# Key norms of a windowed attention: broadcast by matmul, or through memory

## The chip, the cores and the metric

The kernel runs on one core of a Trainium2 chip. The core has TensorE (PE, with weight loads shown apart as PEld), VectorE (DVE), ScalarE (ACT), GpSimd (POOL) and SyncE (SP), which here only issues transfers. The engines run side by side and wait for each other through semaphores; each works through its own instructions in order. SBUF is the core's working memory of 128 partitions (rows), PSUM the memory that TensorE writes to, and beside them lies the device's main memory. The metric is the device's time for one execution in microseconds.

## The reference

x has 2048 tokens of 128 features. It passes through a stack of six layers, then one block of linear attention and feed-forward, then the same stack again with the same weights; each result is added to x, the stack's by half. One layer of the stack is local attention and a feed-forward block with a gate:

```python
def attn_layer(x, Wqkv, qs, ksc, Wo):
    q, k, v = jnp.split(x @ Wqkv, 3, -1)            # 16 heads of 64
    q, k, v = (sh(q), sh(k), sh(v))
    q = l2norm(q) * qs
    k = l2norm(k) * ksc                             # t / max(norm, 1e-12)
    q = q * cos * scale + rotate_half(q) * sin * scale
    k = k * cos * inv + rotate_half(k) * sin * inv
    out = local_attention(q, k, v)                  # windows of 32, one window back
    return out.transpose(0, 2, 1, 3).reshape(b, n, INNER) @ Wo
def ffn_layer(x, g, bln, W1, b1, W2, b2):
    a, gate = jnp.split(layernorm(x) @ W1 + b1, 2, -1)
    return a * gelu(gate) @ W2 + b2
```

The part that matters here is `l2norm(k)`: every key (one head, one token) is divided by its own norm. For the queries the division is done later, in the scale of the exponential.

## The kernel before

Everything is float32 and kept with features on partitions and tokens along the free dimension. Each of the twelve layer passes (`2 * DEPTH`) is cut into eight chunks of `AC` = 256 tokens. A chunk takes four steps, and a step handles 128 tokens and eight heads of attention. The stages of one chunk are:

- `project` (four groups g, L270 on): TensorE projects q and k (p, L286); VectorE multiplies by the rotary tables (prod, L295); GpSimd adds the two halves into the tiles abq and abk (L301); ScalarE squares p (sq, L307) and GpSimd adds the squares (L321). A tile abk holds two groups, thus eight heads: [128, 2, 2, 256]. Its 128 partitions are four heads of 32 rows, the first index is the half of the 64 features, the second the group. There are three buffers of abk.
- `square_sums` (L329): TensorE sums the squares per head and token into ss, with key heads in rows 64 to 71 and 96 to 103.
- `norms` (L400 to L408): ScalarE and VectorE turn ss into the inverse norms rn, one row per head, 256 tokens.
- `query_norms` (L416, L422) brings the query part of rn to the layout rq, tokens on partitions.
- `scale_keys` (L430, L436), for each half g2 of the heads: each key's row of rn has to meet the 32 rows of its head. Two matmuls with a selection matrix of zeros and ones (`sel_r`) write the repeated rows r into two PSUM buffers, and VectorE multiplies abk by them, four heads at a time.
- `gather` (L387, L393): SP copies abq and abk into the layout hq and hk, in which a head's 64 features lie together. For keys it issues four copies per half.
- `similarities` (sim, L466 and L476) on TensorE, with the maxima taken by VectorE (L488, L489); `exponentials` (L501) on ScalarE; `normalised` (L511, L513): a reciprocal on VectorE, a product on GpSimd; `transposed` (te L526, eT L532); `values` (av L553, oT L560 and L562); `output` (y L569, xf L578). `values_windows` copies v into vw with eight DMAs per 128 tokens (L365 to L368).
- `feed_forward` (pf L603, gate L609, h L614, yf L622) runs on 512 tokens, once every eight steps.

The order of work is written out by hand. `POS` gives each stage a list of places (step, position), counted from the first step of its chunk or block; a stage that is a generator is cut at its `yield`s, and each piece has its own place. The pieces of all layers and chunks are sorted by step, then by position, and emitted in that order, so the same order holds on every engine and in SP's queue. Positions only rank the pieces within a step. Semaphores are put in by the framework where data or buffers demand them.

PSUM serves two buffers for sim, one for ss, and five small ones that all other matmul results, r included, take in turn.

Of the kernel before, what the change touches and what calls it, by code (L numbers as in the profile page):

```python
# [8 lines left out]
F32 = mybir.dt.float32  # L9
BF16 = mybir.dt.bfloat16  # L10
AF = mybir.ActivationFunctionType
ALU = mybir.AluOpType
# [3 lines left out]
P = 128  # L16
# [6 lines left out]
CH = 512  # L23
NCH = N // CH
AC = 256
# [5 lines left out]
HID = 512  # L31
LN_EPS = 1e-5
POS = {
    "tabq": [(-10, 141)],
    "tabk": [(-9, 110)],
    "ss": [(-7, 142)],
    "vwin": [(1, 8)],
    "gq0": [(-5, 13)],
    "gq1": [(-3, 49)],
    "e0": [(0, 76)],  # L40
    "e1": [(0, 77)],
    "nrm": [(1, 10)],
    "qn": [(-2, 106)],
    "ek": [(-1, 73)],
    "proj": [(-9, 135), (-8, 33), (-8, 36), (-8, 37), (-8, 39), (-8, 101)],
    "vproj": [(-2, 24), (-2, 71)],
    "norms": [(-4, 38), (-4, 43), (-4, 63)],
    "sk0": [(-3, 69), (-3, 70)],
    "sk1": [(-1, 119), (-1, 136)],
    "te": [(2, 46), (2, 47)],  # L50
    "av": [(2, 132), (2, 177), (2, 178)],
    "out": [(4, 92), (4, 115)],
    "sim": [(0, 50), (0, 53), (0, 54)],
    "ff": [(11, 99), (12, 30), (12, 130), (13, 21), (13, 94), (14, 139), (15, 124), (15, 149),
        (16, 12), (17, 87), (17, 122), (18, 14), (18, 45), (18, 52), (18, 184), (21, 107),
        (21, 167)],
    "ff2": [(12, 15), (12, 80), (13, 95), (14, 58), (14, 60), (14, 79), (15, 91), (16, 40),
        (16, 58), (16, 147), (16, 182), (16, 187), (16, 191), (17, 34), (17, 111), (17, 121),
        (17, 157)],
    "ff3": [(10, 171), (10, 172), (10, 174), (10, 181), (10, 183), (10, 184), (11, 25), (11, 35),  # L60
        (11, 57), (11, 68), (11, 86), (11, 100), (11, 103), (11, 104), (11, 146), (11, 170),
        (11, 170)],
    "start0": [(-16, 180), (-14, 143), (-13, 66), (-11, 67), (-10, 109), (-10, 185)],
    "start1": [(-10, 65), (-9, 134), (-8, 96), (-8, 148), (-6, 20), (-6, 26)],
    "start2": [(-7, 2), (-7, 117), (-6, 6), (-6, 48), (-4, 74), (-4, 176)],
    "start3": [(-6, 28), (-4, 32), (-4, 44), (-4, 75), (-4, 98), (-4, 188)],
    "sums0": [(-9, 105), (-8, 5), (-8, 88), (-8, 123), (-8, 134), (-7, 102), (-7, 118), (-6, 27)],
    "sums1": [(-1, 137), (-1, 145), (0, 56), (0, 114), (1, 116), (1, 133), (2, 154), (2, 172)],
    "sums2": [(1, 189), (2, 173), (2, 178), (2, 192), (3, 144), (3, 153), (4, 125), (4, 126)],
    "sums3": [(3, 179), (4, 11), (4, 19), (4, 42), (4, 82), (4, 83), (4, 84), (4, 128)],  # L70
    "kv": [(5, 1)],
    "outs0": [(5, 3), (5, 4), (5, 7), (5, 9), (5, 22), (5, 85), (6, 18), (6, 113), (6, 164),
        (7, 17), (7, 90), (7, 129), (7, 163), (7, 190)],
    "outs1": [(6, 61), (11, 78), (12, 131), (13, 120), (13, 127), (13, 140), (13, 160), (14, 59),
        (14, 186), (15, 29), (15, 41), (15, 112), (15, 138), (15, 165)],
    "outs2": [(5, 23), (13, 51), (13, 62), (13, 169), (14, 31), (14, 55), (14, 166), (14, 168),
        (15, 44), (15, 64), (15, 159), (16, 150), (16, 158), (17, 97)],
    "outs3": [(5, 175), (15, 93), (16, 16), (16, 81), (16, 151), (16, 160), (16, 161), (17, 72),
        (17, 89), (17, 108), (17, 152), (17, 156), (17, 162), (18, 155)],
}  # L80
EXP_LN = "natural_log_exp_and_others"

# [11 lines left out]
def kernel(ctx: ExitStack, tc: tile.TileContext, a: dict, out: bass.AP):  # L94
    nc = tc.nc

    const = ctx.enter_context(tc.tile_pool(name="const", bufs=1))
    work = ctx.enter_context(tc.tile_pool(name="work", bufs=2))
    ps_sim = ctx.enter_context(tc.tile_pool(name="ps_sim", bufs=2, space=PSUM))
    ps_small = ctx.enter_context(tc.tile_pool(name="ps_small", bufs=5, space=PSUM))  # L100
    ps_ss = ctx.enter_context(tc.tile_pool(name="ps_ss", bufs=1, space=PSUM))

    def small(name):
        return ps_small.tile([P, CH], F32, tag="small", name=name)

    def keep(shape, name, dtype=F32, src=None):
        t = const.tile(shape, dtype, name=name)
        if src is not None:
            dims = "abc"[: len(shape) - 1]
            flat = t.rearrange(f"p {' '.join(dims)} -> p ({' '.join(dims)})") if len(dims) > 1 else t  # L110
            if dtype == F32:
                nc.sync.dma_start(flat, src)
            else:
                nc.sync.dma_start(t, src)
        return t

    def load_qk(l, g):
        w = const.tile([P, 4, P], F32, tag=f"wqk{g}", name=f"wqk{g}_{l}")
        nc.sync.dma_start(
            w,  # L120
            a["Wqk"][l % DEPTH].rearrange("p (g f) -> p g f", g=4)[:, g, :]
            .rearrange("p (u f) -> p u f", u=4),
        )
        return w
# [25 lines left out]
    def load_x(f):  # L150
        nc.sync.dma_start(xo[:, f * CH : (f + 1) * CH], a["xT"][:, f * CH : (f + 1) * CH])

    load_x(0)
    sq_consts = keep([P, 5, P], "sq_consts", src=a["squares"].rearrange("p a b -> p (a b)"))
    ident, hmask, rot_m = (sq_consts[:, i, :] for i in range(3))
    sel_r = sq_consts[:, 3:5, :]
    wqk = [load_qk(0, g) for g in range(4)]
    rot = keep([P, 2, 2, AC], "rot", src=a["rot"])
    qks = keep([P, DEPTH, 2, 2], "qks", src=a["qks"])
# [108 lines left out]
    def chunk(l, c):  # L268
        return chunks.setdefault((l, c), {"nm": f"{l}_{c}"})
# [141 lines left out]
    def query_norms(l, c):  # L411
# [10 lines left out]
        nc.vector.tensor_copy(rq.rearrange("p t h -> p (t h)"), nt[:, 0 : 2 * HEADS])  # L422
        d["rq"] = rq

    def scale_keys(l, c, g2):
        d = chunk(l, c)
        rs = [small(f"r_{d['nm']}_{2 * g2 + i}") for i in range(2)]
        for i in range(2):
            rows = slice(64 + 32 * i, 96 + 32 * i)
            nc.tensor.matmul(  # L430
                rs[i][:, 0:AC], sel_r[rows, g2, :], d["rn"][rows, :], start=True, stop=True
            )
        yield
        for i in range(2):
            k = d["k", g2][:, :, i, :]
            nc.vector.tensor_tensor(  # L436
                k, k, rs[i][:, 0:AC].unsqueeze(1).to_broadcast([P, 2, AC]), ALU.mult
            )
        gather(l, c, "k", g2)

    def earlier_keys(l, c):
# [336 lines left out]
    for l in range(2 * DEPTH):  # L778
        base = per * l + (GAP if l >= DEPTH else 0)

        def put(key, t0, fn, *args):

            places = POS[key]
            if len(places) > 1:
                pieces(fn(*args), t0, places)
            else:
                at(t0 + places[0][0], places[0][1], fn, *args)

        put("tabq", base, tables, l, 0)
        put("tabk", base, tables, l, 1)  # L790
        for c in range(NAC):

            t0 = base + STEPS * c
            for g in range(4):
                put("proj", t0 + g, project, l, c, g)
                put("vproj", t0 + g, values_proj, l, c, g)
            for g2 in range(2):
                put("ss", t0 + 2 * g2, square_sums, l, c, g2)
                put("gq" + "01"[g2], t0, gather, l, c, "q", g2)
                put("sk" + "01"[g2], t0, scale_keys, l, c, g2)  # L800
            for t in range(2):
                put("vwin", t0 + 2 * t, values_windows, l, c, t)
                put("out", t0 + 2 * t, output, l, c, t)
            put("norms", t0, norms, l, c)
            put("qn", t0, query_norms, l, c)
            put("ek", t0, earlier_keys, l, c)
            for s in range(STEPS):
                put("sim", t0 + s, similarities, l, c, s)
                put("e0", t0 + s, exponentials, l, c, s, 0)
                put("e1", t0 + s, exponentials, l, c, s, 1)  # L810
                put("nrm", t0 + s, normalised, l, c, s)
                put("te", t0 + s, transposed, l, c, s)
                put("av", t0 + s, values, l, c, s)
        for f in range(NCH):
            key = "ff"
            if l % DEPTH == DEPTH - 1 and f >= 2:
                key = f"ff{f}"
            put(key, base + 8 * f, feed_forward, l, f)
# [15 lines left out]
def _shape_constants():  # L834
# [7 lines left out]
    t = np.arange(AC, dtype=np.float64)[None, :]  # L842
# [16 lines left out]
    c, s = np.diag(back * np.cos(AC * inv)), np.diag(back * np.sin(AC * inv))  # L859
    one = np.block([[c, -s], [s, c]]).reshape(2, 32, 2, 32).transpose(1, 0, 3, 2).reshape(64, 64)  # L860
    rot_m = np.kron(np.eye(2), one)


    i, j = np.arange(WIN)[:, None], np.arange(SK)[None, :]
# [4 lines left out]
    band = band.reshape(P, 2, SK).astype(ml_dtypes.bfloat16)  # L869
    ident_b = np.tile(np.eye(2 * WIN, WIN), (2, 1)).astype(ml_dtypes.bfloat16)  # L870
    r = np.arange(P)
    sel_r = [r[:, None] % 32 == 4 * i + r[None, :] // 32 for i in range(2)]
    squares = np.stack(
        [r[:, None] == r[None, :], r[:, None] // 8 == r[None, :] // 8, rot_m, *sel_r], 1
    ).astype(np.float32)

    sel = np.zeros((P, 3, 32), np.float32)
# [68 lines left out]
```

## Time and profile before

| | |
|---|---|
| runs, median (lowest to highest) | 3536.89 us (3532.78 to 3539.96) |
| profiled execution, its own time | 3536.21 us |
| its span, first to last instruction | 3534.4 us |
| mean granted TensorE clock | 0.981 of full |
| L430 r, matmul instructions on TensorE | 768, busy 145.1 us |
| L430 r, weight loads | 768, busy 66.8 us |
| L436 abk, VectorE multiplies by r | 384, busy 246.7 us |
| hk<-abk, copies issued by SP | 768 of 128 KB |
| hq<-abq, copies issued by SP | 384 of 256 KB |
| vw<-v, copies issued by SP | 768 of 128 KB, 744 of 64 KB |
| mean DMA traffic over the span | 396.13 MB, 112 GB/s |

Busy time of an engine is the time that at least one of its instructions covers. The ends of matmuls are modelled, while their starts are recorded, and weight loads overlap matmuls. A float32 matmul appears as two instructions. "Idle before" is the time that an engine stood ahead of a group of instructions, with what ended it. SPq is SP's queue of transfer issues.

The twelve passes run in two halves of six, and between them lies the linear attention, where little else can run: there TensorE is busy 294.59 of 372 us (1568 to 1940 us of the span).

### The profile page before, as it was taken

What the parts mean: (1) busy time and instruction counts of PE and PEld (TensorE: products, weight loads), DVE (VectorE), ACT (ScalarE), POOL (GpSimd) and SP (SyncE); (2) the same over time, 40 slices, a digit from 0 to 9 for tenths busy, and PEclk for the clock granted to TensorE, in tenths of its full rate; (3) what the DMA queues carried; (4) which work ended last, traced back from release to release, by engine and by line L of the source; (5) the groups of instructions that cost most, each with busy time, mean ns of one, the idle gap of its engine ahead of it and who ended that gap; (6) DMA issues with size and microseconds to landing.
All of it is one profiled execution on the core that took longest, in us unless ns stands there. A gap on an engine that the chain in (4) does not pass through costs nothing.

```text
span 3534.4 us, 154488 instructions
## 1 busy us (share of the span) xinstructions
PE 3392.8 (96%) x64856; PEld 2346.8 (66%) x64856; DVE 2553.6 (72%) x5116; ACT 2738.4 (77%) x8805; POOL 2092.2 (59%) x2195
## 2 busy tenths in 40 slices
PE   7999999999999999999678999999999999999998
PEld 4776776666776677666335777767667666776674
DVE  5777777777777777775336777777777777777774
ACT  4788788878878878887446787888788788788877
POOL 6766666666666566563136666666666666666661
PEclk9999999999999999999788999999999999999999
DMA  4554544444545455444003544545545454544552
GB/s 123 127 127 119 118 120 117 117 122 120 124 115 126 115 122 131 107 115 104 12 12 83 125 123 123 119 114 126 120 122 120 112 127 119 118 121 117 117 123 61
DMA packets 295921, 396.13 MB, mean 112 GB/s; under 512 B 45501, under 2 KB 160953, under 8 KB 295225
## 3 DMA queue, kind: packets, MB, share of 16 engines
q1 hardware_dynamic: 295224, 386.25, 45.3%
q8 instruction: 510, 8.36, 1.0%
q14 instruction: 187, 1.52, 0.1%
HBM read 34.27 MB, written 1.05 MB: 10 GB/s over the span
## 4 chain that ended last, share of the span: by engine, by line
PE 35%; ACT 8%; DVE 6%; issue 1%; POOL 0%; DMA 0%; ACTq 0%; SPq 0%; POOLq 0%; DVEq 0%
PE p L286 7%; ACT e L501 5%; PE av L553 4%; PE y L569 4%; PE pv L345 4%; DVE prod L295 3%; PE sim L476 3%; PE pf L603 2%; PE yf L622 2%; PE te L526 2%; ACT L607 1%; PE r L430 1%; PE ss L329 1%; PE sim L466 1%; DVE eT L532 1%
## 5 line engine op out<-in xcount | busy, mean ns | idle before, releaser
L501 ACT ACTIVATE e<-sim,st,rq 128x64 f32<-128x64 f32 x3072 | 1194.5, 410 | 292.3 <-DVE st L489 288.9
L295 DVE TENSOR_TENSOR prod<-p,tab 128x1024 f32<-128x1024 f32 x768 | 922.3, 1212 | 130.9 <-ACT sq L307 96.1
L513 POOL TENSOR_TENSOR e<-e,st 128x512 f32<-128x512 f32 x384 | 400.5, 1043 | 724.9 <-DVE st L511 697.6
L286 PE MATMUL p<-xa,wqk 128*128 128x256 f32 x3072 | 773.5, 395 | 18.3 <-ACT sq L307 6.3
L301 POOL TENSOR_TENSOR abq<-prod 128x512 f32<-128x512 f32 x384 | 490.2, 1276 | 297.5 <-DVE prod L295 252.9
L501 ACT ACTIVATION_READ_ACCUMULATOR e<-sim,st,rq 128x1 f32 x3072 | 647.9, 211 | 0.0
L307 ACT ACTIVATE sq<-p 128x512 f32<-128x512 f32 x768 | 438.8, 602 | 248.0 <-PE ss L329 101.4
L286 PEld LDWEIGHTS p<-xa,wqk 128*128 128x128 f32 x3072 | 558.2, 191 | 106.5 <-ACT sq L307 9.6
L301 POOL TENSOR_TENSOR abk<-prod 128x512 f32<-128x512 f32 x384 | 487.2, 1269 | 166.6 <-DVE prod L295 89.5
L321 POOL TENSOR_TENSOR sq<-sq 128x256 f32<-128x256 f32 x768 | 546.9, 734 | 0.0
L553 PEld LDWEIGHTS av<-eT,vw 64*64 64x64 f32 x18432 | 401.7, 135 | 171.3 <-DVE st L489 48.0
L553 PE MATMUL av<-eT,vw 64*64 64x32 f32 x18432 | 446.8, 221 | 3.4 <-issue 1.1
L345 PE MATMUL pv<-wv,xa 128*128 128x512 f32 x768 | 413.4, 620 | 19.4 <-ACT gate L609 18.7
L569 PE MATMUL y<-oT,wo 128*128 128x128 f32 x3072 | 395.1, 282 | 0.2 <-DVE oT L562 0.2
L553 PE MATMUL av<-eT,v 64*64 64x32 f32 x6144 | 390.9, 219 | 0.0
L569 PEld LDWEIGHTS y<-oT,wo 128*128 128x128 f32 x3072 | 359.0, 192 | 19.4 <-issue 1.7
L488 DVE TENSOR_REDUCE sim<-sim 128x4 f32<-128x256 f32 x768 | 325.4, 424 | 14.1 <-PE sim L476 14.0
L476 PE MATMUL sim<-hk,hq 64*32 64x64 f32 x24576 | 332.9, 222 | 0.0
L526 PEld LDWEIGHTS te<-sq_consts,e 128*128 128x128 f32 x1536 | 188.5, 141 | 209.4 <-issue 151.6
L553 PEld LDWEIGHTS av<-eT,v 64*64 64x64 f32 x6144 | 325.6, 135 | 0.0
L476 PEld LDWEIGHTS sim<-hk,hq 64*32 64x32 f32 x24576 | 305.6, 105 | 0.2
L603 PE MATMUL pf<-xc,w 128*128 128x512 f32 (+1 forms) x576 | 290.4, 629 | 11.9 <-POOL xc L591 7.5
(141 smaller groups left out, 4549.6 us busy)
## 6 DMA issues: line engine op xcount, KB each, us to landing
hq<-abq SPq DMA_DIRECT2D x384, 256.0 KB
hk<-abk SPq DMA_DIRECT2D x768, 128.0 KB
vw<-v SPq DMA_DIRECT2D x768, 128.0 KB
vw<-v SPq DMA_DIRECT2D x744, 64.0 KB
wqk<-in_Wqk SPq DMA_DIRECT2D x48, 256.0 KB
wv<-in_Wv SPq DMA_DIRECT2D x24, 256.0 KB
wo<-in_Wo SPq DMA_DIRECT2D x12, 512.0 KB
w<-in_W SPq DMA_DIRECT2D x12, 341.0 KB
```

What stands on the lines that cost most here:

```text
L286: nc.tensor.matmul(both[s][:, u, :], wqk[g][:, 2 * s + u, :], xs, start=True, stop=True)
L295: nc.vector.tensor_tensor(prod, both[s].unsqueeze(2).to_broadcast([P, 2, 2, AC]), tabs[l, s].rearrange("p (u v) t -> p u v t", u=2), ALU.mult,
L301: nc.gpsimd.tensor_tensor(d["qk"[s], g // 2][:, :, g % 2, :], prod[:, 0], prod[:, 1], ALU.add)
L307: nc.scalar.activation(sq, both[s], AF.Square)
L321: nc.gpsimd.tensor_tensor(sq[:, 0, :], sq[:, 0, :], sq[:, 1, :], ALU.add)
L345: nc.tensor.matmul(ps, xa[:, ti * P : (ti + 1) * P], wv[j], start=True, stop=True)
L476: nc.tensor.matmul(sims[par][WIN * b : WIN * b + WIN, i, :], d["hq"][rows, 4 * h8 + i, at : at + WIN], d["hk"][rows, 4 * h8 + i, at : at + ...
L501: nc.scalar.activation(e[:, i, par, :], d["sims", step][par][:, i, :], AF.Exp, bias=st8[:, 0, i, par : par + 1], scale=rq[:, i, par : par ...
L513: nc.gpsimd.tensor_tensor(ef, ef, st8[:, 1].rearrange("p i r -> p (i r)").unsqueeze(2).to_broadcast([P, 8, SK]), ALU.mult,)
L553: nc.tensor.matmul(av[u][r : r + 64, m, WIN * b : WIN * b + WIN], d["vs", t][u][b][:, at : at + DH], d["eT", step][64 * u : 64 * u + 64, i ...
L569: nc.tensor.matmul(y[:, 0:P], wo[:, i, :], d["oT", t].rearrange("p h u m q -> p (h u m) q")[:, i, :], start=(i == 0), stop=(i == 7),)
L603: nc.tensor.matmul(ps[s][:r], w1[:, s, j * P : j * P + r], x, start=True, stop=True)
```

## The change

The inverse key norms no longer pass through TensorE. A new stage, `spread_norms`, writes the two times eight rows of rn that belong to keys into a buffer in main memory (two DMAs), and in a second piece reads them back with four DMAs. Each of the four fills 32 partitions and reads the same 4 KB block for every one of them, so each row is read 32 times. The result is a tile rk of [128, 4, 256] in SBUF, of which there is one buffer; the buffer in main memory exists twice.

`scale_keys` is now a single piece without matmul: one multiply of 128 x 1024 elements per half takes eight heads, both inputs in SBUF. The selection matrices `sel_r` and their part of the load of `squares` are gone. `gather` is called as before.

The table `POS` is written anew as a whole; most pieces keep their step and change their position. Those that stand close to the edit are shown here.

```diff
-    "norms": [(-4, 38), (-4, 43), (-4, 63)],
-    "sk0": [(-3, 69), (-3, 70)],
-    "sk1": [(-1, 119), (-1, 136)],
+    "norms": [(-4, 35), (-4, 75), (-4, 111)],
+    "rk": [(-4, 195), (-3, 19)],
+    "sk0": [(-2, 20)],
+    "sk1": [(-1, 83)],
...
-    "proj": [(-9, 135), (-8, 33), (-8, 36), (-8, 37), (-8, 39), (-8, 101)],
+    "proj": [(-9, 137), (-8, 31), (-8, 32), (-8, 33), (-8, 36), (-8, 57)],
...
-    "sim": [(0, 50), (0, 53), (0, 54)],
+    "sim": [(0, 65), (0, 66), (0, 67)],
...
-    "nrm": [(1, 10)],
+    "nrm": [(1, 9)],
...
-    "start0": [(-16, 180), (-14, 143), (-13, 66), (-11, 67), (-10, 109), (-10, 185)],
+    "start0": [(-18, 189), (-15, 77), (-15, 88), (-15, 140), (-12, 30), (-10, 165)],
...
+    dram = ctx.enter_context(tc.tile_pool(name="dram", bufs=2, space=bass.MemoryType.DRAM))
...
+    def spread_norms(l, c):
+
+        d = chunk(l, c)
+        out = dram.tile([2, 2, 4, AC], F32, tag="rk", name=f"rkd_{d['nm']}")
+        for i in range(2):
+            row = 64 + 32 * i
+            nc.sync.dma_start(out[:, i], d["rn"][row : row + 8, :])
+        yield
+        r = work.tile([P, 4, AC], F32, tag="rk", name=f"rk_{d['nm']}", bufs=1)
+        src = out.rearrange("a b j t -> j (a b) t")
+        for j in range(4):
+            nc.sync.dma_start(
+                r[32 * j : 32 * j + 32], src[j : j + 1].to_broadcast([32, 4, AC])
+            )
+        d["rk"] = r
+
     def scale_keys(l, c, g2):
         d = chunk(l, c)
-        rs = [small(f"r_{d['nm']}_{2 * g2 + i}") for i in range(2)]
-        for i in range(2):
-            rows = slice(64 + 32 * i, 96 + 32 * i)
-            nc.tensor.matmul(
-                rs[i][:, 0:AC], sel_r[rows, g2, :], d["rn"][rows, :], start=True, stop=True
-            )
-        yield
-        for i in range(2):
-            k = d["k", g2][:, :, i, :]
-            nc.vector.tensor_tensor(
-                k, k, rs[i][:, 0:AC].unsqueeze(1).to_broadcast([P, 2, AC]), ALU.mult
-            )
+        k = d["k", g2].rearrange("p u i t -> p u (i t)")
+        r = d["rk"][:, 2 * g2 : 2 * g2 + 2, :].rearrange("p i t -> p (i t)")
+        nc.vector.tensor_tensor(k, k, r.unsqueeze(1).to_broadcast([P, 2, CH]), ALU.mult)
         gather(l, c, "k", g2)
...
+            put("rk", t0, spread_norms, l, c)
```

In program order each engine then meets, for one chunk: VectorE finishes rn (step -4); SP issues the writes at the end of that step and the reads early in the next; VectorE multiplies the first half early in step -2, right behind the reciprocal that stands at the head of the step, and the second half in step -1 behind the maxima of sim; SP issues four copies into hk after each.

## The prediction

> **What bounds the kernel now.** I read the busy table first, then busy time by stretches, then who waits for whom, then single lines of the timeline. The page gives the engines over the whole span:
>
> ```profile
> PE 3392.8 (96%) x64856; PEld 2346.8 (66%) x64856; DVE 2553.6 (72%) x5116; ACT 2738.4 (77%) x8805; POOL 2092.2 (59%) x2195
> ```
>
> An average over stages is not a bound, so here are four stretches (columns: span, then busy time of PE, PEld, DVE, ACT, POOL, then granted clock, DMA share, GB/s). 68 us hold eight steps, that is two chunks of attention and one block of feed-forward.
>
> ```profile
> core 0: us, PE busy (x) PEld busy (x) DVE busy (x) ACT busy (x) POOL busy (x), PEclk, DMA share, GB/s
> 180.00:1568.00 1388.00, 1378.39 (x27448) 971.69 (x27447) 1051.23 (x2119) 1129.33 (x3684) 869.04 (x910) 1.00 0.50 120
> 996.00:1064.00 68.00, 67.60 (x1347) 47.65 (x1348) 51.89 (x104) 55.36 (x182) 42.32 (x45) 1.00 0.46 115
> 1568.00:1940.00 372.00, 294.59 (x3431) 169.74 (x3430) 191.58 (x356) 215.02 (x557) 139.43 (x150) 0.85 0.23 55
> 1940.00:3436.00 1496.00, 1485.59 (x29774) 1050.82 (x29773) 1136.60 (x2297) 1210.73 (x3989) 943.62 (x986) 1.00 0.50 120
> ```
>
> In the two steady stretches, 2884 of 3534 us, TensorE lacks 0.4 us of 68 at the full granted clock; ScalarE has 81%, VectorE 76%, GpSimd 62%. Their idle time ends on TensorE or on each other; in 180 to 1568 us the list of waits has one entry for PE matmuls, 9.3 us in all. TensorE sets the pace there. Around the middle (1568 to 1940) it does not.
>
> **A rule that speaks against this.** The Trainium skill, page "Perfetto Trace Analysis", section "Identifying the Most-Contended Engine", says that matmul busy time is a poor measure since matmuls are pipelined, and to look at the weight loads' share. That share is 70% here, which would leave TensorE headroom and make removed matmuls worth little or nothing. So I do not trust the 96% alone and look at starts, which are not modelled:
>
> ```profile
> 1008.01 0.70 PE L430 MATMUL r<-rn,sq_consts 32*128 32x256 f32 x4
> 1008.64 1.13 PE L603 MATMUL pf<-xc,w 128*128 128x512 f32 x2
> 1027.98 0.70 PE L430 MATMUL r<-rn,sq_consts 32*128 32x256 f32 x4
> 1028.61 0.32 PE L553 MATMUL av<-eT,vw 64*64 64x32 f32 x8
> ```
>
> From the first r matmul to the first of the next group it is 0.63 us both times, behind different neighbours. A fixed spacing is TensorE's own time, not a wait. I go by the row.
>
> **What the change removes on TensorE.** Each scale_keys had four r instructions (two matmuls, two passes each). 768 instructions are 192 groups, and they lie here (busy time of L430 alone):
>
> ```profile
> 180.00:1568.00 1388.00, 60.22 (x324) 27.69 (x324) 1.00 0.50 120
> 1940.00:3436.00 1496.00, 65.74 (x352) 30.38 (x352) 1.00 0.50 120
> ```
>
> (324 + 352)/4 = 169 groups are in the paced stretches: 169 x 0.63 = 106.5 us. The other 23 (14.5 us) lie in the start, middle and end, where TensorE is busy 85, 79 and 83%; I count half, 7 us. Together 113 us. Busy time says 145 us, but its modelled ends overlap the next group, so I take the spacing. The weight loads of r (66.8 us) lie inside it and are not counted again.
>
> **What it does to VectorE.** Removed: 384 multiplies, 246.7 us, and 17.5 us waiting in front of them. Added: 192 multiplies of 128x1024.
>
> ```profile
> L436 DVE TENSOR_TENSOR abk<-abk,r 128x512 f32<-128x512 f32 x384 | 246.7, 684 | 17.5 <-PE r L430 11.4
> L295 DVE TENSOR_TENSOR prod<-p,tab 128x1024 f32<-128x1024 f32 x768 | 922.3, 1212 | 130.9 <-ACT sq L307 96.1 <-PE p L286 30.4 <-POOL e L513 0.9
> ```
>
> The nearest row of that size takes 1.21 us, so 192 x 1.21 = 233 us. But L295 and the old L436 take one input from PSUM; the new multiply has both in SBUF. The Trainium skill, page "SBUF — State Buffer", section "Who interferes with whom", says that such an instruction and a GpSimd instruction that reads SBUF exclude each other, whoever starts second waiting for the first to finish. The trace agrees where it has such a pair:
>
> ```profile
> L242 DVE SCALAR_TENSOR_TENSOR xc<-lnt,xc x48: 691/693/1493, 170.6 to 3515.8; 128x512 f32<-128x512 f32 x48
> L301 POOL TENSOR_TENSOR abk<-prod x384: 1252/1267/1712, 20.3 to 3437.5; 128x512 f32<-128x512 f32 x192
> ```
>
> (minimum/median/maximum). The VectorE row with two SBUF inputs goes from 0.69 to 1.49 us at worst, a GpSimd add from 1.27 to 1.71. Bounds for the new multiply: 1.21 us without a clash, 1.21 + 1.27 = 2.48 with a whole GpSimd add in front. GpSimd is busy 62% of the time, so a random start meets half an add in 62% of cases: 1.21 + 0.62 x 0.64 = 1.6 us. I take 1.6: 307 us instead of 264, VectorE +43 us, and at worst +212. Both are hidden under TensorE: with 192/2884 of it in each us, VectorE goes from 51.9 to some 53 us in an eight-step period that shrinks to 65.5, about 81%. If that cover is gone, +43 us is the price.
>
> **The round trip of the norms.** New per chunk: two writes of 8 KB and four reads of 128 KB, all in SP's queue. One issue takes SP 0.6 us, so 3.6 us more on top of 28 x 0.6 = 17 in a chunk of some 33 us. Bytes: 0.54 MB beside 4.1 MB per chunk (120 GB/s x 34 us), DMA share 0.50 to about 0.58. Neither queue nor engines fill. What counts is latency, since the first read waits for both writes to land, and the first multiply waits for the reads.
>
> ```profile
> 1003.39 0.42 DVE L408 SCALAR_TENSOR_TENSOR rn<-rn,ss 128x256 f32<-128x256 f32 x1
> 1012.72 0.20 DVE L511 RECIPROCAL st<-st 128x8 f32<-128x8 f32 x1 [0.37 <-ACT e L501]
> 1014.72 0.75 DVE L614 SCALAR_TENSOR_TENSOR h<-pf,lvec,gate 128x512 f32<-128x512 f32 x1 [1.80 <-ACT gate L609]
> 2085.34 0.61 SPq L393
> 2086.00 3.78 DMA hk<-abk
> 3531.19 0.34 SPq L638 DMA_DIRECT2D out_xT<-xo  x1
> ```
>
> Four transfers of 128 KB: 0.61 + 3.78 = 4.4 us from the issue that is shown to the landing; the nearest row for the reads. Writes to memory: the only row is the output, issued at 3531.19 with the span ending at 3534.4, so at most 3.2 us, plus 0.6 for the second issue; below, one issue and nothing, 1.2. I take 3.0, nearer to the row. Sum 7.4 us (5.6 to 8.2). The time there is: after.py puts the first multiply behind the reciprocal of the second step after rn. In the timeline of before, rn ends at 1003.81 and that reciprocal at 1012.92, 9.1 us, and this is a pair of short steps; others are longer. So it fits, with 0.9 to 3.5 us over. Behind SP's waiting read stand a pair of hq copies and eight vw copies, wanted by sim and av a step or more later.
>
> If it is late, VectorE stands, and behind the multiply stand the two prod of that step, eT and the maxima that ScalarE waits for. The trace shows what TensorE can bear: VectorE stood 1.80 us before L614 at 1014.72, and TensorE had no gap. The second multiply comes over a step later and is covered.
>
> **What is moved.** The first multiply goes from place (-3, 70) to (-2, 20); the second from (-1, 136) to (-1, 83), so the last hk copies start earlier before sim, which moves from (0, 50) to (0, 65). The first move has a cost: abk has three buffers, and GpSimd's add into the next chunk's second abk, place (-2, 36), must wait until the four hk copies that read the old one have landed. Multiply about 1.6 us, then 4.4: it waits some 2 to 3 us once a chunk. Such waits are 43.5 us in all before. GpSimd has 38% of 34 us, 13 us, to spare per chunk, and sums of squares and exponentials are used over half a step later. I cost it at nothing; with that cover gone, each us is 96 us.
>
> Start: the round trip takes about 7 us where the r matmuls took 1. First r at 43.3 us, first sim at 66.2, so most of it is hidden; I put 4 us for it and for the start of the second half. The rest of the new table of places shifts neighbours without adding work; between -10 and +10 us, taken as 0.
>
> **Sum** on the profiled execution, 3534.4 of span plus 1.8 around it = 3536.2: -113 + 4 = -109, 3427. The median of the runs is 3536.9, 0.7 above, so 3428.
>
> **The rivals.**
> 1. *Part of the gain comes back* (0.17). Clashes of VectorE and GpSimd, or GpSimd's wait for hk, leave TensorE standing about 0.5 us per chunk: 96 x 0.5 = 48 us, 3476. For it: a period of 65.5 us leaves ScalarE 10 us and VectorE 12 of idle time, against 13 and 16 now. Against: before shows that TensorE covers waits of this size.
> 2. *Slower: the round trip is late* (0.19). Place: the first multiply of each chunk. TensorE's idle there must exceed 109/96 = 1.14 us per chunk to cancel the gain; with 1.8 us of cover, the reads must land about 3 us behind the reciprocal, a round trip of some 12 us instead of 7.4. At 13 us TensorE loses about 2.1 us per chunk: 3428 + 202 = 3630; at 12.5 it is about 3580. For it: a write to memory and a read of one 4 KB block by 32 rows are in no row of the trace, and SP takes everything in order. Against: twice my sum for the transfers would be needed.
> 3. *No change* (0.03): another engine takes over at 68 us per period. ScalarE would have to, with 55.4 us of work; 3537.
>
> **Numbers.** The forecast itself has 0.61, range 3405 to 3455 (gain from 121 + 10 to 82). About 0.2% is what can be told from no change, 7 us. Faster: 0.61 + 0.17 = 0.78, within 0.03, slower 0.19. The likeliest is 3428; the range 3403 to 3530 takes in rival 1 and leaves out rival 2 and the edges.
>
> **What would show it.** No L430 rows; an eight-step period of about 65.5 us with TensorE over 99% busy; the multiply at 1.2 to 2.5 us, mean near 1.6; VectorE's waits on DMA rk few and short; GpSimd's waits on hk rising to 200 us or more without TensorE standing. Wrong would be: a long list of VectorE waits on rk, gaps on TensorE behind eT or prod, or a period still near 68 us.

## The result, and the profile after

The changed kernel takes 3645.5 us in the median (3634.1 to 3649.1), the kernel before 3537.0 us beside it. The ratio is 1.0302, 95% interval 1.0277 to 1.0327: about 107 us slower, where 109 us of gain were forecast. In what follows a ratio is turned into microseconds by the 3537 us of before.

The busy table of the page after, and the four stretches of before again (columns: span, busy time of PE, PEld, DVE, ACT, POOL, then granted clock, DMA share, GB/s):

```profile
PE 3328.7 (91%) x64088; PEld 2297.7 (63%) x64088; DVE 2575.6 (71%) x4924; ACT 2748.6 (75%) x8805; POOL 2253.8 (62%) x2195
```

```profile
180.00:1568.00 1388.00, 1315.04 (x26360) 923.82 (x26359) 1030.25 (x1979) 1097.80 (x3573) 913.88 (x886) 0.98 0.54 131
996.00:1064.00 68.00, 65.14 (x1331) 45.97 (x1330) 52.34 (x100) 55.23 (x182) 44.77 (x42) 1.00 0.55 135
1568.00:1940.00 372.00, 289.19 (x3625) 171.25 (x3625) 198.70 (x362) 223.79 (x572) 149.76 (x152) 0.88 0.28 69
1940.00:3436.00 1496.00, 1402.11 (x28201) 984.23 (x28199) 1099.65 (x2118) 1170.67 (x3837) 980.43 (x950) 0.99 0.54 131
```

TensorE lost 64 us of busy time over the span, but it now stands: 1388 - 1315 = 73 us in the first steady stretch, where before it stood 10, and 94 us in the second, also against 10. The granted clock, 1.00 in both stretches before, is 0.98 and 0.99. Over the whole span TensorE is idle 308 us instead of 136 (the idle time in front of its matmuls, summed over the trace). So -64 busy and +172 idle make +108. What it waits for is in GpSimd's groups and in the rows of the new multiply (first lines: busy, mean ns | idle before it, by what ended it; then the multiply's duration minimum/median/maximum, and VectorE's idle before it):

```profile
L302 POOL TENSOR_TENSOR abk<-prod 128x512 f32<-128x512 f32 x384 | 502.4, 1308 | 728.6 <-DMA hk<-abk 573.4 <-DVE prod L296 34.2 <-DVE st L497 25.4
L322 POOL TENSOR_TENSOR sq<-sq 128x256 f32<-128x256 f32 x768 | 593.9, 794 | 0.0
L446 DVE TENSOR_TENSOR abk<-abk,rk x192: 1167/1320/2367, 52.3 to 3573.9; 128x1024 f32<-128x1024 f32 x192
...
  DMA rk<-rkd: 2.1, 3
```

```profile
PE ss L330 <- POOL sq L322: 59.4, 54, 6.8
PE pf L611 <- POOL xc L599: 52.5, 35, 4.6
PE pv L346 <- ACT gate L617: 46.7, 48, 1.8
PE pf L611 <- ACT oT L568: 30.5, 42, 4.4
PE av L561 <- DMA vw<-v: 20.0, 32, 1.3
```

The multiply, once its place comes, waits for the new transfer 2.1 us in all: the round trip itself is on time. GpSimd, though, waits 573 us for the hk copies to leave its abk buffers (before: 43.5 us), 6 us per chunk. Behind that add stand GpSimd's sums of squares and the feed-forward's xc, and for these TensorE waits 59 and 53 us over the whole span. The same waits in the kernel before:

```profile
POOL abk L301 <- DMA hk<-abk: 43.5, 27, 4.1
PE ss L329 <- POOL sq L321: 10.2, 7, 2.7
PE pf L603 <- POOL xc L591: 7.5, 2, 4.6
```

One such place, from the timelines of SP, VectorE and GpSimd in the kernel after (start, duration):

```profile
1003.82 1.43 DVE L446 TENSOR_TENSOR abk<-abk,rk 128x1024 f32<-128x1024 f32 x1
1002.45 1.17 SPq L388 DMA_DIRECT2D hq<-abq  x2
1003.67 0.72 SPq L366 DMA_DIRECT2D vw<-v  x1
...
1009.32 0.59 SPq L369 DMA_DIRECT2D vw<-v  x1
1010.02 2.52 SPq L394 DMA_DIRECT2D hk<-abk  x4
1015.72 1.27 POOL L302 TENSOR_TENSOR abk<-prod 128x512 f32<-128x512 f32 x1 [5.93 <-DMA hk<-abk]
```

The multiply ends at 1005.25, but its hk copies go out at 1010.02, since eight window copies stand ahead of them in SP's queue, and those stood behind the hq copies, which wait for sim (573.7 us of SP's waiting over the span). GpSimd's add, for which the buffer must be free, comes at 1015.72 after 5.93 us of standing. Over all chunks the median time from the end of the multiply to the issue of its first hk copy is 1.69 us for the first half of the heads and 4.70 us for the second. Before, SP stood ready: its first copy goes out 0.57 us ahead of the end of the pair of multiplies.

### The profile page after: what moved, and what is told of

Its sections match the earlier page's. It is cut to its first block, busy times and chain, and to the rows that moved or that the text cites. A ratio compares the mean times of both kernels' runs of the same rounds, so it can differ in the third digit from the quotient of the medians.

```text
span 3642.3 us, 153352 instructions
## 1 busy us (share of the span) xinstructions
PE 3328.7 (91%) x64088; PEld 2297.7 (63%) x64088; DVE 2575.6 (71%) x4924; ACT 2748.6 (75%) x8805; POOL 2253.8 (62%) x2195
## 4 chain that ended last, share of the span: by engine, by line
PE 47%; ACT 17%; DVE 13%; POOL 9%; DMA 7%; issue 4%; SPq 4%; POOLq 0%; ACTq 0%; DVEq 0%
PE p L287 10%; ACT e L509 9%; DVE prod L296 6%; PE av L561 6%; PE y L577 6%; PE pv L346 4%; PE pf L611 4%; DMA hk<-abk 4%; PE sim L484 4%; PE yf L630 3%; POOL abk L302 3%; POOL sq L322 3%; PE te L534 3%; SPq L394 2%; DMA vw<-v 2%
## 5 line engine op out<-in xcount | busy, mean ns | idle before, releaser
L302 POOL TENSOR_TENSOR abk<-prod 128x512 f32<-128x512 f32 x384 | 502.4, 1308 | 728.6 <-DMA hk<-abk 573.4
L287 PE MATMUL p<-xa,wqk 128*128 128x256 f32 x3072 | 782.1, 398 | 7.9 <-DVE xa L243 4.0
L521 POOL TENSOR_TENSOR e<-e,st 128x512 f32<-128x512 f32 x384 | 475.7, 1239 | 288.7 <-DVE st L519 223.0
L302 POOL TENSOR_TENSOR abq<-prod 128x512 f32<-128x512 f32 x384 | 508.0, 1323 | 178.7 <-DVE prod L296 160.0
L322 POOL TENSOR_TENSOR sq<-sq 128x256 f32<-128x256 f32 x768 | 593.9, 794 | 0.0
L611 PE MATMUL pf<-xc,w 128*128 128x512 f32 (+1 forms) x576 | 304.2, 655 | 84.4 <-POOL xc L599 52.5
L570 DVE COPY oT<-av 128x256 f32<-128x256 f32 x384 | 162.1, 422 | 255.1 <-PE av L561 252.5
```

The lines of the kernel that those rows point to most:

```text
L287: nc.tensor.matmul(both[s][:, u, :], wqk[g][:, 2 * s + u, :], xs, start=True, stop=True)
L302: nc.gpsimd.tensor_tensor(d["qk"[s], g // 2][:, :, g % 2, :], prod[:, 0], prod[:, 1], ALU.add)
L322: nc.gpsimd.tensor_tensor(sq[:, 0, :], sq[:, 0, :], sq[:, 1, :], ALU.add)
L521: nc.gpsimd.tensor_tensor(ef, ef, st8[:, 1].rearrange("p i r -> p (i r)").unsqueeze(2).to_broadcast([P, 8, SK]), ALU.mult,)
L611: nc.tensor.matmul(ps[s][:r], w1[:, s, j * P : j * P + r], x, start=True, stop=True)
```

## The experiments

The runs tell these theories apart. Theory A: the new table of places makes the hk copies late in SP's queue. Theory T or L: the round trip costs, by its transfers and SP's time (T), or because something is late through it (L). Theory G: ScalarE's gate is the next bound, right behind TensorE, so that removed matmuls bring little. Theory P, called B in the first expectations: VectorE and GpSimd hold each other up. Theory C: the added transfers fill the DMA engines. G was formed after the first four runs, whose expectations don't speak of it. The short diffs are against the kernel named ahead of them.

**e1_vw_places**, against after: the window copies behind the hk copies.

```diff
-    "vwin": [(1, 68)],
+    "vwin": [(0, 21)],
```

> The changed kernel with one place moved: the eight vw copies go from place (1, 68) to (0, 21), so that they no longer stand in SP's queue right ahead of the hk copies. Theory A (the hk copies start late because of what stands ahead of them in SP's order, the abk buffers come free late, GpSimd waits, TensorE starves): from the end of the multiply to the first hk issue 1.7 and 4.7 us fall to under 1 us, GpSimd's wait for hk falls from 575 us to under 250, time 3430 to 3520. Theory B (VectorE's multiply with two SBUF inputs and GpSimd shut each other out): nothing of that matters, 3620 to 3650. Theory C (the added transfers fill the DMA engines): 3620 to 3650.

Measured 3578.2 us, ratio 1.0113 (1.0098 to 1.0128). The first hk copy now goes out 0.03 us after the multiply, GpSimd's wait for hk falls from 573 to 124 us, and 67 us come back, which neither B nor C foresaw:

```profile
POOL abk L302 <- DMA hk<-abk: 124.0, 99, 3.4
```

The direction of A is right and its size was too large: 40 us above before remain, and the 109 us of gain are still missing.

**e2_matmul_at_places**, against after: the matmuls and the multiplies from PSUM at the new places, no round trip.

```diff
-    "rk": [(-4, 195), (-3, 19)],
-    "sk0": [(-2, 20)],
-    "sk1": [(-1, 83)],
+    "sk0": [(-2, 19), (-2, 20)],
+    "sk1": [(-1, 82), (-1, 83)],
```

> The changed kernel's table of places, but with the r matmuls and the two multiplies from PSUM of the kernel before, and no round trip through memory. Theory A (places and SP's order are the cause): still slow, 3600 to 3700, GpSimd's wait for hk above 400 us. Theory B (port) and C (transfers): both causes are gone, so 3530 to 3560.

Measured 3782.3 us, 1.0685 (1.0667 to 1.0703), GpSimd's wait for hk 393 us: slower than A's range, the wait just under its 400. The new places are bad for the old method too, worse by 137 us than with the round trip. So the new transfers can't be the whole cause. Why it is worse still was not taken apart; TensorE waits in front of r for the gate (66.9 us) and for the multiplies (32.8 us), and its clock is lower (last section).

**e3_trip_old_places**, against before: the round trip and the multiply of eight heads, at the old places.

```diff
-    "sk0": [(-3, 69), (-3, 70)],
-    "sk1": [(-1, 119), (-1, 136)],
+    "rk": [(-4, 64), (-4, 65)],
+    "sk0": [(-3, 71)],
+    "sk1": [(-1, 136)],
```

> The kernel before with its own places, and of the change only the round trip and the one multiply of eight heads: writes at (-4, 64), reads at (-4, 65), first multiply at (-3, 71), second at (-1, 136). Theory A: GpSimd's wait for hk stays under 200 us and the time is 3425 to 3480. Theory B and C: the multiply and the transfers are all there, so 3600 to 3660.

Measured 3693.0 us, 1.044 (1.042 to 1.046): a miss. Here the multiply does wait for the transfer (rows of the round trip's tile):

```profile
L446 DVE TENSOR_TENSOR abk<-abk,rk x192: 1224/1472/5870, 51.9 to 3621.8; 128x1024 f32<-128x1024 f32 x192
...
  DMA rk<-rkd: 73.0, 54
```

VectorE stands in every second chunk, and there it is 7.7 us in the median from the end of rn to the multiply: that is the length of the round trip. The old places leave 6.1 us in these chunks, as e8 shows below.

**e4_no_trip_old_places**, against e3: no round trip, the multiply by a constant tile.

```diff
-    "rk": [(-4, 64), (-4, 65)],
-        r = d["rk"][:, 2 * g2 : 2 * g2 + 2, :].rearrange("p i t -> p (i t)")
+        r = ones[:, 2 * g2 : 2 * g2 + 2, :].rearrange("p i t -> p (i t)")
```

> The kernel before with its own places, the r matmuls left out, and one multiply of eight heads by a constant tile in SBUF; the division of the keys by their norms is left out. It measures what the r matmuls are worth, with the new multiply and without any round trip. By the prediction's sum for TensorE 3415 to 3435. Theory B: above 3500 in spite of that. If the removed matmuls were worth nothing: 3537.

Measured 3522.7 us, 0.9958 (0.9943 to 0.9973), as theory B forecast; e5 and e6 ask whether its reason holds. The hk copies aren't late here (GpSimd waits 43.6 us for them, as before), 768 matmuls are gone, and the kernel gains 15 us, not 109. TensorE waits for the gate now, 64.2 us over the span against 18.7 before; the waits of e4 from 400 to 1500 us (in all, times, longest), a window of 4 us in it, and ScalarE's timeline in that place:

```profile
PE pv L346 <- ACT gate L601: 26.3, 31, 1.5
```

```profile
1008.00:1012.00 4.00, 2.55 (x15) 1.13 (x15) 1.28 (x4) 3.95 (x11) 1.90 (x2) 1.00 0.49 100
```

```profile
1009.52 1.28 ACT L599 ACT_TABLE_LOAD   x1
1010.82 0.69 ACT L601 ACTIVATE gate<-pf,lvec 128x512 f32<-128x512 f32 x1
1011.52 1.28 ACT L604 ACT_TABLE_LOAD   x1
```

ScalarE is full for these 4 us (3.95) while TensorE stands 1.45. The gate of 0.69 us is led in and out by a table load of 1.28 us, and the matmul pv waits for one of the five small PSUM buffers, which pf holds until the gate has read it.

**e5_no_multiply**, against e4: the multiply is left out as well.

```diff
-        nc.vector.tensor_tensor(k, k, r.unsqueeze(1).to_broadcast([P, 2, CH]), ALU.mult)
```

> The old places without round trip (3522.7 us) and now without the multiply of the keys as well; the keys are not divided by their norms. Theory G (with the r matmuls gone, the feed-forward's gate on ScalarE is the next bound, since the matmuls pv wait for a PSUM buffer that the gate frees): VectorE's 315 us of multiplies were hidden, so 3505 to 3525 us, TensorE's wait for the gate stays near 26 us in 400 to 1500 us. Theory P (the multiply with two SBUF inputs and GpSimd's squares hold each other up, and this took TensorE's gain): the squares go back from 961 to some 710 ns and the time falls to 3425 to 3480 us.

Measured 3497.5 us, 0.9891 (0.9876 to 0.9906). GpSimd's squares go from 961 to 736 ns, so VectorE and GpSimd do hold each other up there, but that is worth only 24 us with the multiply's own time; P's 3425 to 3480 isn't reached, G's 3505 to 3525 is missed by 8 us, and TensorE still waits 33.6 us for the gate between 400 and 1500 us. P thus has a small part in it and not the large one.

**e6_no_table_loads**, against e4, and **e10_before_no_tables**, the same edit on the kernel before:

```diff
-            nc.scalar.preload_act_table_set("gelu_and_others")
-                gate[:r], ps[1][:r], AF.Gelu, bias=lvec[:r, l, 6 + j : 7 + j]
+                gate[:r], ps[1][:r], AF.Square, bias=lvec[:r, l, 6 + j : 7 + j]
-            nc.scalar.preload_act_table_set(EXP_LN)
```

> The old places without round trip (3522.7 us), with a square in place of the feed-forward's gelu and without the two table loads around it (what is computed in the feed-forward is thus another function). Theory G: ScalarE gets back 2 x 1.28 us in each feed-forward step, the gate frees its PSUM buffer earlier, and TensorE's gain of 109 us comes out: 3420 to 3460 us, the period of eight steps near 65.5 us. If ScalarE's gate is not the next bound: 3505 to 3525 us.

> The kernel before with a square in place of the feed-forward's gelu and without the two table loads around it (another function is computed there). Theory G (TensorE sets the pace, ScalarE's gate stands close behind it): with the r matmuls in place TensorE stays full, so 3490 to 3530 us; the distance to the same edit without the r matmuls (3393.2 us) is what they are worth when ScalarE is out of the way, 100 to 130 us. If ScalarE was the bound before as well: 3390 to 3430 us, and the matmuls are worth next to nothing in any case.

Measured 3393.2 us, 0.960 (0.9585 to 0.9614), and 3492.3 us, 0.9887 (0.987 to 0.9903). e10 is in G's range. e6 is below its own of 3420 to 3460, which left out that the edit is worth 40 us in the kernel before too. With ScalarE out of the way the same removal of matmuls is worth 2.9%, 102 us by the ratios, 99 by the medians; with ScalarE as it is, 15. The windows 180 to 1568 us, of e10 and of e6:

```profile
180.00:1568.00 1388.00, 1384.33 (x27704) 971.04 (x27703) 1070.56 (x2141) 974.48 (x3591) 878.30 (x917) 1.00 0.50 121
```

```profile
180.00:1568.00 1388.00, 1377.99 (x28373) 980.47 (x28372) 1126.38 (x2136) 1020.52 (x3737) 990.21 (x946) 1.00 0.53 126
```

TensorE is over 99% busy in both, at the full clock, and weight loads are at 70% and 71%. G is shown: the row of 0.63 us per group gave the right size for TensorE, but only if nothing else comes next. The edit takes 370 us off ScalarE's busy time and frees the gate at once, so it doesn't tell the gate from ScalarE's load as a whole.

**e8_trip_unread**, against e3: all six transfers stay, the multiply reads a constant tile.

```diff
-        r = d["rk"][:, 2 * g2 : 2 * g2 + 2, :].rearrange("p i t -> p (i t)")
+        r = wlin[:, 512 * g2 : 512 * g2 + 512]
```

> The old places with the round trip (3693.0 us), all six transfers kept, but the multiply reads a constant tile and so waits for none of them; the keys are not divided by their norms. Theory L (the round trip cost time there because the multiply, and with it the copies of hk and GpSimd's add, came late): 3520 to 3560 us. Theory T (SP's six issues per chunk, their wait for the writes, or the transfers themselves cost it): 3650 to 3700 us. Between: both.

Measured 3569.5 us, 1.010 (1.0085 to 1.0115). Of the 170 us between e4 and e3 by the ratios, 120 go to the multiply being late and 50 to the six transfers alone, so both L and T have a part. The 50 look like SP's order again: SP stands for rn and for the writes, and GpSimd waits for the hq copies behind them (e4: 17.1 us); that nothing else in the transfers costs is not shown. The rows are from the waits of SP and GpSimd in e8:

```profile
SPq L432 <- DVE xf L586: 480.0, 91, 7.4
...
SPq L437 <- DMA rkd<-rn: 109.9, 127, 1.3
```

```profile
POOL abq L302 <- DMA hq<-abq: 177.4, 55, 5.9
```

(The first wait is put down to VectorE's instruction next to rn.)

**e9_trip_sk0_later** and two more places for the round trip, against e3:

```diff
-    "rk": [(-4, 64), (-4, 65)],       # e3
-    "sk0": [(-3, 71)],
+    "sk0": [(-3, 150)],               # e9, rk as in e3
+    "rk": [(-3, 50), (-3, 51)],       # e12_behind_windows
+    "sk0": [(-2, 11)],
+    "rk": [(-3, 9), (-3, 10)],        # e16_trip_ahead_of_hq
+    "sk0": [(-2, 11)],
```

> The old places with the round trip, the first half's multiply moved from place 71 to place 150 of its step, some 3.4 us later. Theory L: VectorE's wait for rk goes from 73 us to under 10, and the time falls to 3530 to 3600 us, with GpSimd's wait for hk some 100 to 200 us. Theory T: 3660 to 3700 us.

> The old places with the round trip, its six transfers queued on SP behind the window copies and the second half's hq copies instead of ahead of them, and the first half's multiply one reciprocal later on VectorE (behind the row that ends near 1012.9 us in the kernel before, 9.1 us after the norms). Theory L with theory G: nothing is late any more, VectorE's wait for rk under 10 us, and the time is that of the old places without a trip plus little: 3520 to 3575 us. If the transfers as such cost time: 3600 to 3690 us.

> The old places with the round trip, its six transfers queued on SP behind the eight window copies but ahead of the second half's hq copies, which wait for the similarities; the first half's multiply stands behind the reciprocal as in the run with the trip behind the hq copies (3735.8 us). Theory L: the trip is on time (VectorE's wait for rk under 20 us), the hq copies come some 6 us later than in the kernel before, 3540 to 3600 us. If lateness isn't the cause of that run's loss: 3690 us or more.

Measured 3655.8 us, 1.0346 (1.0326 to 1.0366); 3735.8 us, 1.0573 (1.0557 to 1.0589); 3639.3 us, 1.0299 (1.0282 to 1.0315). All three forecasts missed. In e9 the place was later, but in the chunks that wait VectorE has nothing to do between the two places, so the multiply came at the same point (7.6 us after rn) and waited 69.7 us in all. In e12 SP met the hq copies first, which wait for sim; the trip's first write went out a median 4.5 us after rn in every second chunk, 1.5 in the others, and VectorE waited 204.7 us:

```profile
L446 DVE TENSOR_TENSOR abk<-abk,rk x192: 1173/1460/4679, 51.9 to 3668.5; 128x1024 f32<-128x1024 f32 x192
...
  DMA rk<-rkd: 204.7, 75
```

In e16, ahead of those hq copies but behind the earlier hk ones, it still waited 91.1 us. What failed in the last two is one assumption, that SP reaches a place of the queue in time; in e9 it was that a later place is a later time.

**e13_no_trip_new_places** and **e14_no_trip_vw_places**: after and e1 without the round trip, with the edit of e4.

> The changed kernel with its own places, the round trip left out, the multiply by a constant tile; the keys are not divided by their norms. Theory A1 (the new places alone, with eight window copies ahead of the hk copies, make the copies late): 3610 to 3650 us, GpSimd's wait for hk stays above 450 us. Theory A2 (the round trip on SP, which stands until the norms are there, is what pushes the window copies and with them hk back): without it SP runs ahead again, GpSimd's wait for hk falls under 200 us and the time to 3530 to 3590 us.

> The changed kernel with the window copies moved behind the hk copies (3578.2 us), now also without the round trip, the multiply by a constant tile; the keys are not divided by their norms. Theory A2: the trip still costs there, 3510 to 3550 us. Theory A1: the trip is hidden there and what is left lies in the places and in ScalarE's gate, 3565 to 3580 us.

Measured 3562.2 us, 1.0085 (1.0066 to 1.0105), and 3545.7 us, 1.0022 (1.0004 to 1.0039). Neither A1 nor A2 holds alone: without the trip GpSimd still waits 459 us for hk (A2 said under 200; row below), the second half's hk copies still go out 4.36 us after the multiply, while the first half's lateness is gone (0.03 us); but the time falls as A2 said. The second half's lateness comes with the places, the first half's with the trip. At the new places the trip costs 77 us, with the window copies moved 32.

```profile
POOL abk L302 <- DMA hk<-abk: 459.1, 150, 7.4
```

**e11_after_no_tables** and **e15_vw_no_tables**: after and e1 with the edit of e6.

> The changed kernel with a square in place of the feed-forward's gelu and without the two table loads around it (another function is computed there). Theory A (the copies of hk come too late at the new places, whatever ScalarE does): 3490 to 3590 us, GpSimd's wait for hk stays at 400 us or more. If ScalarE's gate alone took the gain: 3380 to 3430 us as with the old places.

> The changed kernel with the window copies moved behind the hk copies (3578.2 us), with a square in place of the feed-forward's gelu and without the two table loads around it (another function is computed there). Theory G (what was left of the gain there went into ScalarE's gate, where TensorE waited 29.5 us between 400 and 1500 us): 3420 to 3480 us. If SP's order still holds it back, as in the changed kernel with the same edit (3565.5 us): 3520 to 3560 us.

Measured 3565.5 us, 1.0081 (1.0058 to 1.0103), and 3453.6 us, 0.9774 (0.9758 to 0.979). In e11 SP's order holds everything up whether ScalarE is full or not (A; GpSimd waits 639.5 us for hk). In e15, where the hk copies are not held back, G's forecast is met.

| ScalarE as it is | no round trip | with round trip |
|---|---|---|
| matmuls, old places (before) | 3537 | |
| old places | 3522.7 (e4) | 3693.0 (e3), unread 3569.5 (e8) |
| new places | 3562.2 (e13) | 3645.5 (after) |
| new places, window copies behind hk | 3545.7 (e14) | 3578.2 (e1) |

| without table loads | no round trip | with round trip |
|---|---|---|
| matmuls, old places | 3492.3 (e10) | |
| old places | 3393.2 (e6) | |
| new places | | 3565.5 (e11) |
| new places, window copies behind hk | | 3453.6 (e15) |

None of the kernels run here that divide the keys by their norms and keep the gelu is faster than the one before. Of the runs with the changed method, only the one with both its copies in better order and ScalarE relieved gains: e15 is 1.1% faster than e10 (0.9774 against 0.9887).

## Why the prediction was wrong

By the ratios, the way from before to after is -15 us (matmuls out, eight heads at a time, old places: e4), +45 (the new places: e13), +77 (the round trip at them): +107. The forecast was -113 + 4 = -109. Of the 216 us between them, 98 lie in the first term and 45 and 77 in terms that were put at nothing, less the 4. The split holds for this order of steps: with ScalarE relieved the first term is worth about 100, and places and round trip together cost 170 (e11 against e6).

*Removed on TensorE, -113.* The term has nearly the right size where TensorE alone sets the pace (-99 to -102, e6 against e10), and nearly vanishes in this kernel (-15). The step that failed is "TensorE sets the pace there", read from windows of 68 us and more, in which ScalarE has 81%, and taken to hold once the matmuls are out. For the kernel before it is nearly true: ScalarE relieved gains 40 us there (e10). But within the period the bound changes. The same view of the kernel before, cut to 4 us, shows it:

```profile
1012.00:1016.00 4.00, 3.60 (x19) 1.97 (x19) 1.83 (x4) 3.94 (x8) 1.04 (x1) 1.00 0.84 171
```

ScalarE is full (3.94 of 4), TensorE stands 0.40, up to a pv at 1014.74. This is the place of which the prediction says "TensorE had no gap", so its 1.8 us of cover rest on a wrong reading. And the one entry in its list of waits, 9.3 us in all, is this gate:

```profile
PE pv L345 <- ACT gate L609: 9.3, 26, 0.4
```

The third rival, that ScalarE takes over at 68 us per period, had the right mechanism for this term and 0.03 of chance, since it was weighed by the 55.4 us of the whole period.

*The rule that spoke against the change* (the Trainium skill, page "Perfetto Trace Analysis", section "Identifying the Most-Contended Engine") would have made the removed matmuls worth little, and in e4 they were. But its reason, headroom seen in a weight loads' share of 70%, isn't what the runs show: at the same share in e10 TensorE was the bound, and taking the matmuls away there gave about 100 us. The row was the better guide to TensorE; it is silent on who is next.

*VectorE +43, hidden.* The multiply was put at 1.6 us; its mean is 1.40 after (267.9 us in all), 1.64 in e4. That it is hidden was nearly right: leaving it out gave 24 us (e5). GpSimd's squares grew from 734 to 794 ns, in e4 to 961. That is on the side of the rule of the Trainium skill's page "SBUF — State Buffer", section "Who interferes with whom", at a small price.

*The round trip, 7.4 us.* Where the multiply waits on it, 7.7 us from rn (e3); after leaves 9.1 us in every second chunk and 11.5 in the others (medians), and VectorE waits 2.1 us in all. From the first write's issue to the first read's it is 2.5 us (1012.63 to 1015.14 in after), where 3.0 was assumed. That part was right, and the second rival, the late round trip, did not occur at the places chosen; it is what e3, e9, e12 and e16 show. The six issues take SP 3.1 us, against 3.6 in the prediction. Wrong was the sentence next to it, that behind SP's waiting read "stand a pair of hq copies and eight vw copies, wanted by sim and av a step or more later". What stands behind those is the hk copies, and these free GpSimd's buffer. Without the trip the first half's copies go out 0.03 us after the multiply instead of 1.69, and GpSimd's wait falls from 573 to 459 us (e13); how much of the +77 that makes isn't shown.

*What is moved: "I cost it at nothing".* This is the second step that failed. The wait of GpSimd was put at 2 to 3 us a chunk, by a multiply and four copies at once; it is 6 us, because the copies are not issued when the multiply ends. Nor is it covered: TensorE stands 172 us more, with 94 of them in front of ss and pf for GpSimd's sums and xc. The price put on lost cover, 96 us for each us, was too high: 530 us more of GpSimd's waiting went with those 172. Moving the window copies alone gives back 67 us with the round trip, 22 without it.

*The other places, 0 within 10.* All new places together cost 45 us without the round trip; 22 of them lie in the window copies, the other 23 (e14 against e4) were not taken apart.

*Start +4.* The first sim starts 3.3 us later than before, as forecast, but the one that starts at 183.3 us in before is 14.3 us late in after (in e4 it is 4.5 us late). So the start loses nearer to 14.

The first rival had the mechanism, "GpSimd's wait for hk, leave TensorE standing", with half a us per chunk; all that TensorE stands more is 172/96 = 1.8 us.

What stays open: four abk buffers, which might take GpSimd's wait away directly, were not tried, nor a further small PSUM buffer for the gate's wait. Nor is it shown how the round trip's 77 us divide between SP standing for rn, SP's issues and the later hq copies.

## What to carry to other kernels

Before an engine's removed work is counted as gain, look at the same stretch in windows as short as one stage: who is full there, and which buffer does it hold that the relieved engine needs next? A transfer queued in order costs what stands behind it, not only its own latency; go down the queue from its place to the first copy that frees a buffer. And an order of work that fits one method doesn't fit another: the old matmuls at the new places cost 245 us, the new transfers at the old ones 156.

## What the runs showed of the hardware

*Idle time of TensorE, even in short gaps, costs clock.* From 180 to 1568 and from 2000 to 3436 us of the kernel before, TensorE has no gap over 0.41 us and no time below full clock. After has 48 gaps of over 1 us there, and 18 stretches of 3.41 us at half clock. One of them, TensorE's timeline and the window around it in after:

```profile
331.84 3.60 PE L611 MATMUL pf<-xc,w 128*128 128x512 f32 x4 [2.74 <-POOL xc L599]
```

```profile
331.00:335.00 4.00, 3.16 (x4) 1.18 (x4) 2.81 (x6) 2.84 (x15) 4.00 (x5) 0.59 0.68 169
```

Four instructions of pf take 3.60 us after a gap of 2.74 us, at a granted clock of 0.59. The Trainium skill, page "TensorE: Matmul & The Clock Gate", section "HAM oscillation — how this bites in real kernels", gives as the rule that TensorE must not idle for more than about 3.4 us. Here shorter gaps were enough, so the measurement decides, but not every one was: 31 of the 48, the longest of 2.83 us among them, were followed by no half clock. The length of a gap is not what separates them. In each trace these stretches begin on a grid of 3.413 us. Cut all 17 traces along their grids, in the same parts of the span, and look at the pieces at full clock: where TensorE stood under 1 us of a piece, the next piece was never at half clock (0 of 6730); from 1 to 2 us it was in 112 of 515 cases; from 2 us on always (130 of 130). So a gap that falls across two pieces can go free, and two short ones in one piece can cost.

Inside such a stretch a pf matmul starts 0.853 us after the one before it, outside 0.429 (medians): half speed. The 18 stretches (61 us) thus cost at most 31 us. In e3 they are 188 us and in e2 198, so at most 94 of its 156 us of loss and 99 of its 245. A wait on TensorE's path can thus be dearer than its own length.
